# Sixteen offloaded quarter tiles spread over fourteen states, in place of four whole states, in a fused Mamba decoder kernel

## The chip, the cores and the metric

One core of one Trainium2 chip runs the whole program in a single launch. The metric is the device time of that launch in microseconds (us); the time before is the median of three runs. The engines are named as in the profile: PE is TensorE, PEld its weight loads, DVE VectorE, ACT ScalarE, POOL GpSimd and SP the queue that issues most DMAs.

## The reference, cut to what matters

A decoder layer over 4 sequences of 1024 tokens, width 512: a Mamba block with a gated MLP, a cross-attention, and a feed-forward layer with routed low-rank experts, each added to its input and layer-normalised. The change lies in the Mamba block's selective scan, which has 1024 channels and 16 states:

```python
dA = jnp.exp(jnp.einsum('bld,dn->bldn', dt, A))
dBu = jnp.einsum('bld,bln,bld->bldn', dt, Bm, u_act)
def step(h, inputs):
    dA_t, dBu_t = inputs
    h = dA_t * h + dBu_t
    return (h, h)
y = jnp.einsum('lbdn,bln->bld', hs, Cm) + u_act * Dp
```

The last line is the sum over the 16 states n of `hs * C`. Which engine adds which piece of that sum is all that the change touches. Everything is 32-bit.

## The kernel before, in words

**Blocks.** The 4096 tokens are cut into 8 chunks `c` of 512 tokens, and the 1024 channels into 2 halves of 4 blocks of 128. One chunk and one half make a group `g` of 16 states `n`; there are 16 groups, numbered 0 to 15. A group is even for the first half of its chunk and odd for the second half. So there are 256 state positions `k`, and each has four slots `q`. A slot is one call of `quarter(k, q, other)`. Every engine's instructions are chained in the order in which the program writes them (the wrapper `InOrder`, whose helper is line 289 of the profile). Only DMA issues on SP are placed by the tile scheduler.

**What a slot holds.** In slot (k, q) the program writes, in this order: four transposes on PE (`turn`, tile `ps_h`, 128 tokens of the four channel blocks of state k-1); some PE work of another stage (`other`); one scan on DVE (`scan`, 128x512, the q-th channel block of state k); one exponential on ACT (`exp`, tile `da`, for the scan two slots later; `da` has two buffers); `times_c` for the quarter tile t = q of state k-1, which multiplies the transposed tile by C and adds it to the accumulator `acc`; and in slots 0 and 1 a product on POOL (`times_b`, tile `hs`, 128x1024, half of the input of state k+1; `hs` has three buffers). From the second token chunk of a sequence on, ACT also adds the carried state to the first column of `hs`.

**Three ways of adding.** `times_c` takes one of these ways, by state:

- state 0: ACT writes `acc` (one instruction);
- state 15 (`JS`): ACT writes C times the tile into a buffer `hc`, and PE later sums `acc` and `hc` when it transposes back;
- states in `AS`: ACT writes `hc` (six buffers), and one slot later POOL adds `hc` to `acc`;
- all others: one DVE instruction, `acc = ps * c + acc`.

The POOL addition is put into phase 3 of the next slot, so it is queued after the product `times_b` that this slot holds. For t = 3 it lands between the two products of a position; for t = 0 behind the second; for t = 1 and 2 in slots that hold no product. As the sums of state n run one position late, a state n in `AS` frees DVE at position n+1: positions 5, 8, 11 and 14.

**The other stage.** In groups 0 and 1, `other` is the rest of the input projection. From group 2 on it is the MLP of the chunk before, metered at 1.9 units of PE work per slot; a unit is three matmuls (`ps_ab`, `ps_m`), one step of the output projection (`ps_o`) or four transposes (`ps_t`). The output projection of a chunk starts at a fixed slot, number 18 of an even group (position 4, slot 2), and takes 32 units. Behind it stands a chain over several engines: the sum of squares on ACT, a small reciprocal square root on POOL (`ss`, `rs_r`, `rs_w`, `nr`), a scaling on ACT (`hn`), transposes on PE (`ps_t`), and a split on ACT and DVE (`xn`). Each product pair of the MLP also gives DVE two instructions on `g`, ACT a tanh and a cast, and POOL a subtraction (`gs`).

**After the scan.** The last two chunks' MLP and the attention follow (from about 2577 us of the span). The change leaves their instructions as they are.

Of the kernel before, what the change touches and what calls it, by code (L numbers as in the profile page):

```python
# [126 lines left out]
LOADS = {(8, 0): [(0, 1), (0, 0)], (14, 1): [(1, 1)], (15, 0): [(1, 0)]}  # L127
FG = 4

AS = (4, 7, 10, 13)  # L130
JS = (15,)
H, DK, SK = 16, 32, 64
E, R = 8, 16
# [539 lines left out]
def scan_mlp(tc, cn, a, dr, before, bx, then):  # L673
# [8 lines left out]
    with ExitStack() as ctx, ExitStack() as sx:  # L682
# [12 lines left out]
        class Step:  # L695
# [79 lines left out]
            def times_c(self, t):  # L775

                c = cts[self.c][:, t, self.n : self.n + 1]
                ps = self.ps.rearrange("p i d -> p (i d)")
                if self.n == 0:
                    acc = accs[self.g, t] = ap.tile([P, GJ * P], F32, tag="acc", name="acc")  # L780
                    nc.scalar.activation(acc, ps, AF.Copy, scale=c)
                elif self.n in AS + JS:
                    acc = accs[self.g, t]
                    hc = yp.tile([P, GJ * P], F32, tag="hc", name="hc", bufs=6)
                    nc.scalar.activation(hc, ps, AF.Copy, scale=c)
                    if self.n in AS:
                        at(1, 3, nc.gpsimd.tensor_tensor, acc, acc, hc, ALU.add)
                    else:
                        hcs.setdefault((self.g, t), []).append(hc)
                else:  # L790
                    acc = accs[self.g, t]
                    nc.vector.scalar_tensor_tensor(acc, ps, c, acc, ALU.mult, ALU.add)
# [40 lines left out]
        def at(d, phase, f, *args):  # L833

            due.setdefault((now[0] + d, phase), []).append(lambda: f(*args))
# [218 lines left out]
        n = NC * 2 * NS  # L1054
# [961 lines left out]
```

## Time and profile before

| what | value |
|---|---|
| median of three runs | 3428.85 us (3427.82 to 3434.39) |
| profiled execution, its own time | 3433.46 us |
| its span | 3431.7 us |
| groups 0 and 1 (569.9 to 793.6 us) | 223.7 us |
| even groups 4 to 14, one each | 128.7 to 135.4 us |
| odd groups 3 to 15, one each | 121.0 to 124.7 us |

The profile is that of one execution. A group's bounds are the starts of its first scan and of the next group's first scan on DVE. An engine's busy time in a stretch is the union of its instructions; DVE instructions overlap a little at their ends, so the cost of one to the queue is the distance between starts. A wait is put down to what came last before the waiting instruction.

### The profile page before, as it was taken

To read this page: it belongs to the slowest core of one execution; us is meant where nothing else is said; L and a number is where in the kernel's file an instruction comes from. 1 tells how busy PE (TensorE), PEld (TensorE's weight loads), DVE (VectorE), ACT (ScalarE), POOL (GpSimd) and SP (SyncE) were. 2 spreads that over 40 slices of the span, in tenths; PEclk is the share of its full clock that TensorE was granted. 3 is DMA by queue.
4 is the path that set the end of the run, shared out by engine and by line. 5 is a ranking of instruction groups with operands and counts; after the bars stand their busy time and mean duration, and the time that the engine had idled before them with its cause. 6 is when DMAs were issued, how large, how long until landed. Compare 5 with 4: busy or idle time off the path is not lost. (4 is left out here: it accounts for less than half of the span.)

```text
span 3431.7 us, 46914 instructions
## 1 busy us (share of the span) xinstructions
PE 3015.1 (88%) x15504; PEld 2369.0 (69%) x15504; DVE 2962.6 (86%) x4169; ACT 1982.9 (58%) x3894; POOL 2487.0 (72%) x2177
## 2 busy tenths in 40 slices
PE   7888885567898899899899899899899997999986
PEld 5666663344775776776776776776776787998875
DVE  6989999999999998998998998998993446888887
ACT  4666666555665655665555665656662335666642
POOL 1455447898998998998998998998993115667642
PEclk9999996567998999999999999999999999999998
DMA  4666645333655765665755665765657642111110
GB/s 163 217 240 226 240 167 176 132 111 121 195 176 180 220 189 186 215 193 185 222 186 182 214 190 179 221 188 187 202 177 236 178 129 90 32 56 50 42 37 31
DMA packets 478473, 562.77 MB, mean 164 GB/s; under 512 B 46006, under 2 KB 309814, under 8 KB 477974
## 3 DMA queue, kind: packets, MB, share of 16 engines
q1 hardware_dynamic: 464406, 526.21, 48.0%
q10 hardware_dynamic: 13824, 33.56, 2.7%
q8 instruction: 123, 2.02, 0.2%
q14 instruction: 120, 0.98, 0.1%
HBM read 430.18 MB, written 129.50 MB: 163 GB/s over the span
## 5 line engine op out<-in xcount | busy, mean ns | idle before, releaser
L289 POOL TENSOR_TENSOR hs<-pk,b 128x1024 f32<-128x1024 f32 x512 | 1213.9, 2391 | 61.8 <-issue 26.3
L289 DVE TENSOR_TENSOR_SCAN hs<-da,hs 128x512 f32<-128x512 f32 x1024 | 1220.4, 1208 | 15.6 <-ACT da L289 14.5
L289 ACT ACTIVATE da<-pk,aneg 128x512 f32<-128x512 f32 x1024 | 706.9, 691 | 734.1 <-DVE hs L289 726.5
L289 PE MATMUL ps_h<-ident,hs 128*128 128x128 f32 x4096 | 716.5, 299 | 190.0 <-DVE hs L289 128.1
L289 PEld LDWEIGHTS ps_h<-ident,hs 128*128 128x128 f32 x4096 | 549.8, 153 | 432.6 <-DVE hs L289 158.1
L289 PE MATMUL ps_ab<-xn,w 128*128 128x512 f32 x3072 | 837.7, 408 | 4.0 <-DVE xs L289 3.4
L289 PEld LDWEIGHTS ps_ab<-xn,w 128*128 128x128 f32 x3072 | 546.8, 191 | 99.4 <-DVE xs L289 4.1
L289 DVE SCALAR_TENSOR_TENSOR acc<-ps_h,c,acc 128x512 f32<-128x512 f32 x640 | 465.3, 727 | 63.3 <-PE ps_h L289 49.7
L289 PE MATMUL ps_m<-w,gs 128*128 128x512 f32 x1536 | 424.0, 411 | 8.0 <-POOL gs L289 5.5
L289 POOL TENSOR_TENSOR acc<-acc,hc 128x512 f32<-128x512 f32 x256 | 325.6, 1286 | 39.2 <-ACT hc L289 39.1
L289 PEld LDWEIGHTS ps_m<-w,gs 128*128 128x128 f32 x1536 | 277.2, 193 | 59.8 <-POOL gs L289 8.9
L289 PE MATMUL ps_o<-wo,wy 128*128 128x512 f32 x512 | 242.4, 598 | 0.3 <-DMA wo<-in_w_out_dram 0.3
L289 POOL TENSOR_TENSOR gs<-g,gs 128x512 fp32r<-128x512 f32 x128 | 165.1, 1290 | 103.6 <-ACT gs L289 101.6
L289 ACT ACTIVATE hc<-ps_h,c 128x512 f32<-128x512 f32 x320 | 216.0, 675 | 17.5 <-PE ps_h L289 17.2
L289 PE MATMUL ps_in<-xn,wu 128*128 128x512 f32 x768 | 220.3, 436 | 0.7 <-ACT xn L450 0.4
L289 PE MATMUL ps_in<-xn,wz 128*128 128x512 f32 x768 | 192.2, 398 | 3.0 <-ACT wz L147 2.4
L289 PEld LDWEIGHTS ps_in<-xn,wu 128*128 128x128 f32 x768 | 148.8, 195 | 62.0 <-issue 25.5
L289 POOL TENSOR_TENSOR pt<-pw,pt 128x512 fp32r<-128x512 f32 x48 | 64.6, 1345 | 150.3 <-ACT pt L289 117.2
L289 PEld LDWEIGHTS ps_in<-xn,wz 128*128 128x128 f32 x768 | 142.6, 188 | 36.8 <-ACT wz L147 2.8
L289 DVE SCALAR_TENSOR_TENSOR g<-g,ps_ab 128x512 f32<-128x512 f32 x128 | 86.5, 676 | 85.4 <-ACT g L289 83.8
L289 DVE SCALAR_TENSOR_TENSOR cv<-ps_in,pvec,cv 128x509 f32<-128x509 f32 (+2 forms) x192 | 143.2, 746 | 4.8
L289 POOL TENSOR_TENSOR r<-r,e 128x512 f32<-128x512 f32 x64 | 92.1, 1444 | 68.8 <-DVE e L289 43.1
(247 smaller groups left out, 4891.5 us busy)
## 6 DMA issues: line engine op xcount, KB each, us to landing
w<-w SPq DMA_DIRECT2D x384, 512.0 KB, 5.3
b<-b SPq DMA_DIRECT2D x256, 256.0 KB, 4.0
pk<-pk SPq DMA_DIRECT2D x64, 512.0 KB, 7.4
w<-pt SPq DMA_DIRECT2D x48, 512.0 KB, 3.3
pk<-z SPq DMA_DIRECT2D x64, 256.0 KB, 2.2
pk<-u SPq DMA_DIRECT2D x32, 512.0 KB, 3.5
pk<-r SPq DMA_DIRECT2D x32, 512.0 KB, 3.9
pk<-q SPq DMA_DIRECT2D x32, 512.0 KB, 4.4
```

Of the source, the lines that this page charges most:

```text
L289: ins = f(*args, **kw)
```

## The change

`AS` becomes a set of pairs (state, quarter tile) in place of four states, and `times_c` looks up the pair:

```diff
-AS = (4, 7, 10, 13)
+
+AS = {(n, t) for n in range(1, 15) for t in range(4) if (4 * (n - 1) + t) * 16 % 56 < 16}
...
-                elif self.n in AS + JS:
+                elif (self.n, t) in AS or self.n in JS:
                     acc = accs[self.g, t]
                     hc = yp.tile([P, GJ * P], F32, tag="hc", name="hc", bufs=6)
                     nc.scalar.activation(hc, ps, AF.Copy, scale=c)
-                    if self.n in AS:
+                    if self.n not in JS:
                         at(1, 3, nc.gpsimd.tensor_tensor, acc, acc, hc, ALU.add)
```

The pairs are (1,0), (2,0), (2,3), (3,3), (4,2), (5,2), (6,1), (7,1), (8,0), (9,0), (9,3), (10,3), (11,2), (12,2), (13,1), (14,1): sixteen in each group, four for every t, as before. States 0 and 15 stay as they were. No instruction is added or removed on any engine; on DVE, ACT and POOL the ones of this sum change places, PE's order is the same, and on SP some loads swap with their neighbours.

## The prediction

> **What bounds the kernel now.** I read the engine shares first, then busy time by group, then by state position in an even and an odd group, then what DVE waits for, then single instructions on DVE and POOL. The page's line for DVE:
>
> ```profile
> DVE  6989999999999998998998998998993446888887
> ```
>
> Each digit is a fortieth of the span, in tenths. From slice 6 to slice 29, where the scan runs beside the other stages, DVE is at 8 or 9. The scan phase is therefore near DVE's limit, and what is left is in the eights. Busy time by group (columns: us, then PE, PEld, DVE, ACT, POOL busy with instruction counts, PE clock, DMA share, GB/s), for groups 8 to 11:
>
> ```profile
> 1548.50:1681.80 133.30, 118.93 (x585) 86.63 (x584) 120.78 (x143) 71.76 (x131) 116.74 (x83) 0.95 0.55 175
> 1681.80:1804.10 122.30, 117.19 (x650) 96.05 (x650) 119.00 (x139) 73.44 (x132) 115.10 (x75) 1.00 0.71 218
> 1804.10:1939.50 135.40, 120.81 (x586) 86.46 (x585) 121.24 (x144) 82.78 (x183) 117.33 (x85) 0.95 0.55 177
> 1939.50:2064.10 124.60, 117.36 (x650) 96.08 (x649) 119.03 (x139) 82.76 (x174) 114.70 (x72) 1.00 0.71 219
> ```
>
> DVE has the same work in both kinds. An odd group leaves it idle for 122.3 - 119.0 = 3.3 us: nothing but DVE bounds it. An even group leaves it idle for 133.3 - 120.8 = 12.5 us. That idle time is the stake. By state position, same columns, in group 8: positions 5 to 9, 11 and 12, and then position 5 of group 9:
>
> ```profile
> 1587.50:1592.60 5.10, 5.10 (x21) 2.75 (x20) 5.10 (x7) 4.14 (x9) 2.94 (x3) 1.00 0.82 237
> 1592.60:1603.00 10.40, 10.40 (x41) 5.56 (x40) 7.93 (x10) 4.30 (x9) 9.38 (x7) 1.00 0.12 36
> 1603.00:1610.70 7.70, 7.70 (x31) 4.21 (x30) 7.70 (x10) 3.35 (x8) 5.88 (x4) 1.00 0.11 36
> 1610.70:1616.80 6.10, 6.10 (x25) 3.32 (x24) 5.22 (x7) 4.44 (x10) 6.10 (x4) 1.00 0.08 29
> 1616.80:1627.90 11.10, 11.10 (x53) 7.49 (x52) 7.90 (x11) 4.91 (x10) 8.88 (x6) 1.00 1.08 317
> ...
> 1636.20:1642.20 6.00, 6.00 (x38) 5.06 (x36) 5.86 (x8) 5.09 (x11) 6.00 (x4) 1.00 0.54 164
> 1642.20:1655.50 13.30, 7.76 (x38) 6.03 (x35) 10.59 (x14) 7.12 (x13) 13.30 (x9) 0.74 0.20 60
> ```
> ```profile
> 1723.20:1728.80 5.60, 5.60 (x33) 4.62 (x32) 5.60 (x7) 4.03 (x8) 5.17 (x5) 1.00 0.30 102
> ```
>
> Positions 5, 8 and 11 are those where a whole state is off DVE. In the even group PE is busy for all of positions 5 to 9 (40.4 of 40.4 us): this is the output projection. There DVE runs through position 5 in 5.1 us and then waits at position 6; the same happens at 8 and 9. Two of the four offloaded states free DVE where PE is the bound. At positions 11 and 12 POOL is busy throughout (19.3 of 19.3 us). In the odd group DVE is busy for all of position 5, so an offload there is fully used. What DVE waited for in group 8 (waiting, what ended it, us, times, longest):
>
> ```profile
> DVE acc L289 <- PE ps_h L289: 7.2, 6, 2.9
> DVE acc L289 <- POOL acc L289: 2.3, 1, 2.3
> ```
>
> And the POOL one in order of time, first on DVE, then on POOL:
>
> ```profile
> 1633.14 0.72 DVE L289 SCALAR_TENSOR_TENSOR acc<-ps_h,c,acc 128x512 f32<-128x512 f32 x1
> 1633.78 1.21 DVE L289 TENSOR_TENSOR_SCAN hs<-da,hs 128x512 f32<-128x512 f32 x1
> ...
> 1642.18 1.22 DVE L289 TENSOR_TENSOR_SCAN hs<-da,hs 128x512 f32<-128x512 f32 x1
> 1645.72 0.75 DVE L289 SCALAR_TENSOR_TENSOR acc<-ps_h,c,acc 128x512 f32<-128x512 f32 x1 [2.31 <-POOL acc L289]
> ```
> ```profile
> 1639.76 4.71 POOL L289 TENSOR_TENSOR hs<-pk,b 128x1024 f32<-128x1024 f32 x2
> 1644.43 1.25 POOL L289 TENSOR_TENSOR acc<-acc,hc 128x512 f32<-128x512 f32 x1
> ```
>
> From these starts I take the cost of one sum to DVE's queue: 1633.78 - 1633.14 = 0.64 us (its record says 0.72, but its end overlaps the next start). The stall shows POOL, late, holding up the first sum of state 11.
>
> **The change, part by part.** Work is the same on every engine: 16 offloads a group, before and after. Only the places differ, so the sum goes by place.
>
> *Up to the output projection, even groups 2 to 14.* Before position 5, the old kernel had no offload. The new one has four: (1,0) runs at position 2, (2,0) and (2,3) at 3, (3,3) at 4. Positions 3 and 4 are DVE's (its busy time is all of 7.8 and 7.1 us in group 8), so three of these shorten them: 3 x 0.64 = 1.9 us. The one at position 2 I take as worth nothing: DVE waited there for PE anyway. The projection's start is fixed by slot, so it comes 1.9 us sooner. Inside, PE's pace holds: DVE needs about 7.1 + 0.7 - 0.6 = 7.2 us a position (four scan-and-sum pairs of 1.13 + 0.64, one MLP instruction, less one sum) against PE's four slots of 2.16 us between successive groups of `ps_h`, 8.6 us. Five offloads instead of eight lie there, and the three that leave cost nothing. 7 x 1.9 = 13.5 us gained. Bounds: 0, if the projection's start hangs on something else, to 7 x 2.6.
>
> *Behind the projection, even groups.* POOL's order up to the second product for position 12 was h, two products, `gs`, two products; it becomes h, two products, add, `gs`, product, add, product. Two adds of 1.25 us come ahead: the first product of position 12 ends at about 1643.4 instead of 1642.1, the second at 1647.0 instead of 1644.4. DVE loses three free sums at position 11 (one stays), so in group 8 it gets to position 12 at 1636.2 + 4 x 1.13 + 3 x 0.64 + 2 x 0.6 = 1643.9, just after the product. The sum that stalled is then ready, and the third scan of position 12 starts at about 1649.4; before, it started at 1650.15. That is 0.8 us gained in groups 4, 8 and 12. The same count in group 10, where DVE waited only 0.54 us for that add, gives 0.35 us lost in groups 6, 10 and 14. Together -1.3 us. One add fewer stands ahead of the `gs` that ended a wait of PE (1.36 us) at position 13, behind which DVE waited 0.67 to 0.78: I take 0.7 off in six groups, 4.2 us. Bounds a group: +1.8 (see the POOL rival) to -3.6 (all idle time of DVE from position 10 to 13 gone).
>
> *Odd groups.* DVE is busy nearly throughout, and 16 x 0.64 us are saved wherever they lie. PE must hold without DVE's fast positions: it needs 4 x 1.83 = 7.3 us a position (start to start of `ps_h` beside two MLP units), DVE 7.1 + 1.2 - 0.6 = 7.7 with two MLP instructions. POOL's products were ready 2.5 us or more ahead of their scans at positions 10 to 13, so one add more in between is covered. Value 0; bounds -1.5 (half of the idle 3.3) to +0.9 (three light positions at PE's pace).
>
> *Groups 0 and 1.* DVE is busy 218.3 of 223.7 us. Value 0, bounds -4 to +2.
>
> *ACT and SP.* ACT's sixteen `hc` (0.67 us) go from bursts of four to singles; ACT is busy below 70% in every group, and `da` has two slots of lead. If that cover failed, each would cost its 0.67 us on a scan. The swapped loads on SP are taken at nothing: no DMA heads a wait of DVE above 0.4 us in groups 8 and 9.
>
> [...] In the trace the adds took 1254/1289/1327 ns (least, median, most) and DVE's sums 720/723/753 between 1200 and 2400 us, so neither waits on the other. [...]
>
> *Sum.* -13.5 - 1.3 - 4.2 = -19 us. Against the profiled execution's own 3433.5 us (span 3431.7 and 1.8 around it) that is 3414.5. The median of the runs is 4.6 us lower, so I forecast 3428.85 - 19 = 3410 us, 0.55% less. Some 0.2%, 7 us, is what a measurement can tell from no change.
>
> **The rivals.** *Smoothing pays everywhere (0.12).* If no engine meets a burst any more, even groups lose 1.9 + 3.6 = 5.5 us and odd ones 1.5: 7 x 5.5 + 7 x 1.5 = 49, near 3380. For it: three engines each have 116 to 121 us of work in 133. Against: the projection stays PE's.
>
> *Nothing moves (0.15).* If POOL and PE, not DVE, set where the projection starts, the 13.5 us are not gained, and the rest is within 6 us. For it: POOL is busy for all of positions 1 and 2 of group 8. Against: positions 3 and 4 are all DVE.
>
> *POOL decides at positions 11 to 13 (0.22), slower.* The products have no lead there (first scan at 1636.22, product done just before). Two adds ahead and a third, (10,3), between the next two delay the chain by 3 x 1.25 = 3.75 us in each even group, against 1.9 gained: 7 x 1.85 = +13, 3442 us. It decides if POOL gets there more than 0.5 us later against DVE than I count.
>
> **How the numbers follow.** My forecast has 0.51. It spreads by 10 us, so 0.47 of it is a gain above 7 us and 0.04 none. With the first rival, faster is 0.59; with the second, the same is 0.19; the third makes slower 0.22. The range, 3384 to 3439, reaches from near the smoothing case to short of the POOL case; about 0.2 is left out.
>
> **What would show it.** Right: even groups shorter by about 2 to 3.5 us, odd ones within 1; positions 3 and 4 shorter by three sums; DVE's wait for POOL's `acc` gone; `ps_o` still without gaps. Wrong: waits of DVE or ACT for POOL's `hs` at positions 11 to 13, odd groups longer with DVE waiting for `ps_h`, or adds above 1.33 us.

## The result

The kernel after takes 3437.64 us (median of 20 runs, 3432.16 to 3440.41) against 3430.07 us for the kernel before on the same chip (20 runs): 1.0019 times the time before by the means, with an interval of 1.0012 to 1.0026. It is slower by some 6.5 us (7.6 us between the medians) where 19 us of gain were forecast.

The profiled execution of after took 3432.16 us, span 3430.4. It is the fastest of its runs. The scan phase (groups 0 to 15) grew from 2007.4 to 2012.7 us. What lies around it, the same instructions in both, took 1424.3 us in the one profile and 1417.7 in the other, and between 1417.7 and 1426.9 in all profiles of this study. So the profiles are used below for places, and the medians for what a kernel costs.

The page of after, DVE's row by fortieths of the span:

```profile
DVE  6989999998999998998999999999993446888887
```

The row is as full as before. Groups 8 to 11 by windows (us, then PE, PEld, DVE, ACT and POOL busy with instruction counts, PE clock, DMA share, GB/s):

```profile
1552.30:1686.00 133.70, 118.67 (x585) 86.94 (x584) 120.91 (x143) 72.08 (x131) 117.48 (x92) 0.96 0.56 178
1686.00:1809.60 123.60, 118.03 (x650) 96.00 (x649) 118.94 (x140) 72.83 (x132) 114.34 (x66) 1.00 0.69 215
1809.60:1943.90 134.30, 121.46 (x585) 89.08 (x584) 120.99 (x143) 82.95 (x183) 117.86 (x94) 0.92 0.57 178
1943.90:2067.60 123.70, 117.99 (x650) 96.02 (x649) 118.97 (x139) 81.96 (x174) 113.73 (x64) 1.00 0.70 218
```

The even groups still leave DVE idle for 12.8 and 13.3 us, the odd ones for 4.7: the idle time that was the stake is all there. The next windows are positions 4 to 9, 11, 12, 14 and 15 of group 8, then positions 3 and 5 of group 9:

```profile
1583.70:1590.10 6.40, 5.27 (x22) 4.26 (x23) 6.40 (x8) 3.36 (x6) 6.40 (x5) 0.73 0.77 261
1590.10:1597.90 7.80, 7.80 (x34) 4.55 (x33) 7.17 (x10) 5.29 (x10) 6.86 (x5) 1.00 0.66 199
1597.90:1606.40 8.50, 8.50 (x33) 4.46 (x32) 7.30 (x9) 3.81 (x8) 5.29 (x3) 1.00 0.12 39
1606.40:1614.20 7.80, 7.80 (x32) 4.28 (x31) 7.28 (x10) 3.70 (x8) 7.80 (x6) 1.00 0.04 15
1614.20:1622.80 8.60, 8.60 (x33) 4.59 (x32) 7.33 (x9) 4.15 (x9) 8.49 (x6) 1.00 0.24 55
1622.80:1631.30 8.50, 8.50 (x44) 6.11 (x43) 7.11 (x9) 3.60 (x8) 5.33 (x3) 1.00 1.09 325
...
1639.70:1649.80 10.10, 6.33 (x35) 4.51 (x34) 7.69 (x9) 4.80 (x10) 10.10 (x6) 1.00 0.64 181
1649.80:1659.90 10.10, 6.95 (x38) 5.88 (x37) 9.79 (x13) 7.35 (x14) 10.10 (x7) 0.83 0.18 50
...
1669.20:1677.60 8.40, 6.91 (x38) 5.34 (x37) 8.37 (x12) 3.50 (x6) 7.81 (x4) 1.00 0.85 291
1677.60:1686.00 8.40, 7.51 (x41) 6.06 (x40) 8.37 (x12) 3.90 (x7) 6.93 (x19) 1.00 0.92 308
...
1709.80:1719.30 9.50, 7.61 (x46) 6.17 (x44) 7.08 (x9) 3.59 (x7) 9.50 (x6) 1.00 1.10 326
...
1726.90:1734.60 7.70, 7.49 (x41) 6.02 (x41) 7.70 (x11) 4.54 (x8) 5.75 (x4) 1.00 0.37 124
```

Positions 5 to 9 are even now, and PE fills them (41.2 of 41.2 us; 40.4 before): the projection is still PE's. At position 11 DVE works for 7.69 of 10.10 us while POOL is full. At 14 and 15 DVE is full, as it was before, when the two took 15.6 us and not 16.8:

```profile
1666.30:1672.80 6.50, 6.01 (x35) 4.82 (x34) 6.47 (x10) 4.21 (x7) 4.36 (x4) 1.00 0.82 247
1672.80:1681.90 9.10, 8.21 (x45) 6.60 (x44) 9.06 (x14) 4.38 (x9) 8.45 (x11) 1.00 1.06 374
```

In group 9, position 5 is DVE's as before, but position 3 leaves it idle for 2.4 us. What DVE waited for in group 8:

```profile
DVE acc L290 <- PE ps_h L290: 5.3, 11, 1.4
DVE y L290 <- PE ps_y L290: 3.7, 3, 1.6
DVE acc L290 <- POOL acc L290: 2.4, 1, 2.4
DVE hs L290 <- POOL hs L290: 1.1, 1, 1.1
```

The wait for POOL's `acc`, 2.3 us before, is still there, with a wait for POOL's `hs` beside it. In order of time, DVE and then POOL:

```profile
1639.72 1.22 DVE L290 TENSOR_TENSOR_SCAN hs<-da,hs 128x512 f32<-128x512 f32 x1 [1.07 <-POOL hs L290]
1643.33 0.75 DVE L290 SCALAR_TENSOR_TENSOR acc<-ps_h,c,acc 128x512 f32<-128x512 f32 x1 [2.38 <-POOL acc L290]
```
```profile
1632.25 0.19 POOL L290 TENSOR_SCALAR ss<-ss 128x4 f32<-128x4 f32 x1 [4.12 <-ACT carry L290]
...
1636.04 1.29 POOL L290 TENSOR_TENSOR h<-h,hn 128x512 f32<-128x512 f32 x1
1637.29 4.76 POOL L290 TENSOR_TENSOR hs<-pk,b 128x1024 f32<-128x1024 f32 x2
1642.00 1.29 POOL L290 TENSOR_TENSOR acc<-acc,hc 128x512 f32<-128x512 f32 x1
```

The stall has moved one position ahead, from the first sum of state 11 to the first of state 10: it waits for the add of (9,0) into the same accumulator, which POOL reaches behind the norm's chain (`ss` to `nr`), `h` and two products.

Where the time went, by stretch of a group, as means of the seven profiled groups of a kind (starts of first scans, as in the views above):

| stretch | before | after | change | forecast |
|---|---|---|---|---|
| even, positions 0 and 1 | 12.88 | 13.47 | +0.59 | 0 |
| even, 2 to 4 | 25.23 | 23.34 | -1.89 | -1.9 |
| even, 5 to 9 (projection) | 40.60 | 41.09 | +0.49 | 0 |
| even, 10 to 13 | 37.96 | 37.71 | -0.25 | -0.8 |
| even, 14 and 15 | 15.37 | 16.62 | +1.25 | not counted |
| odd, 0 to 3 | 33.52 | 32.90 | -0.62 | 0 (whole group) |
| odd, 4 to 15 | 89.26 | 90.11 | +0.85 | |

The 0.59 us of positions 0 and 1 lie in groups 2 and 4 alone (2.2 and 2.0 us). Group 2 comes up again below; in group 4 DVE waits 1.7 us for ACT's `da`, which it did not before, and why stays open. The last group is counted up to the end of its last scan.

### The profile page after: what moved, and what is told of

Read it like the earlier page. It is cut to its first block, busy times and chain, and to the rows that moved or that the text cites. A ratio compares the mean times of both kernels' runs of the same rounds, so it can differ in the third digit from the quotient of the medians.

```text
span 3430.4 us, 46766 instructions
## 1 busy us (share of the span) xinstructions
PE 3012.5 (88%) x15504; PEld 2370.4 (69%) x15504; DVE 2961.4 (86%) x4169; ACT 1981.4 (58%) x3894; POOL 2486.5 (72%) x2177
## 4 chain that ended last, share of the span: by engine, by line
PE 39%; DVE 35%; issue 9%; DMA 7%; ACT 5%; POOL 4%; SPq 0%; ACTq 0%; DVEq 0%; POOLq 0%
DVE hs L290 12%; DVE acc L290 7%; PE ps_ab L290 7%; PE ps_o L290 7%; PE ps_m L290 5%; PE ps_in L290 4%; PE ps_h L290 4%; PE ps_s L290 3%; PE ps_b L290 2%; DVE g L290 2%; DVE cv L290 2%; POOL hs L290 2%; DMA uz<-pk 2%; DVE h L290 1%; PE ps_y L290 1%
```

## The experiments

Theory: the change is the sum of a gain ahead of the projection and of new waits behind single instructions in POOL's and SP's queues. Rivals, by run: the gain is not there; the loss is one and the same everywhere; POOL is simply full. A function `offload(g)` gives the set of pairs by group; WHOLE is the set of before and SPREAD that of after. All ratios are to the kernel before on the same chip; 0.001 is 3.4 us.

**Which groups lose.** Three runs with SPREAD in one kind of group only, WHOLE in the others.

```diff
-                elif (self.n, t) in AS or self.n in JS:
+                elif (self.n, t) in offload(self.g) or self.n in JS:
# x1_odd:   SPREAD if g > 2 and g % 2 else WHOLE
# x2_even:  SPREAD if g >= 2 and g % 2 == 0 else WHOLE
# x3_first: SPREAD if g < 2 else WHOLE
```

> The spread set in the odd groups from 3 on, whole states elsewhere. Theory A (odd groups are DVE's before and after, so it does not matter where the sixteen sums lie): within 3 us of the kernel before; the seven odd groups of the two profiles differ by +1.7 us together. Rival B (without whole states DVE loses its run ahead, and each position costs the greater of PE and DVE): 5 to 8 us slower, with waits of DVE for ps_h in the odd groups.

> The spread set in the even groups from 2 on, whole states elsewhere. Theory A (what positions 3 and 4 save is capped by PE, which runs there at a granted clock of about 0.75, and the stall on POOL's sum moves from position 12 to position 11): within 4 us of the kernel before. My forecast's reading was 19 us faster. Rival B (the whole loss of the changed kernel lies here): 5 to 8 us slower.

> The spread set in groups 0 and 1 alone, beside the input projection, whole states elsewhere. Theory A (POOL is late for its products in group 1 once single sums stand among them; the two profiles differ by +2.3 us there): 2 to 6 us slower, the greater part of what the changed kernel loses. Rival B (the loss lies in the even or odd groups): within 2 us of the kernel before.

Measured: x1 3439.46 us, 1.0027 (1.0016 to 1.0037); x2 3427.61, 0.9987 (0.9979 to 0.9996); x3 3436.70, 1.0019 (1.0009 to 1.0029). The even groups gain some 4 us (by the profiles nothing: +0.2 us a group in the table), far short of 19; the odd ones lose 9 and groups 0 and 1 lose 6, where the forecast had nothing. The three add up to 11 us against 6.5 for the whole change, within their intervals. Rival B of x1 has the sign and nearly the size, but not its cause: DVE's long wait in the odd groups of x1 is for a `uz` load (below), not for `ps_h`.

**The three early sums.** After, with (2,0), (2,3) and (3,3) left on DVE in even groups from 2 on.

```diff
+    return SPREAD - {(2, 0), (2, 3), (3, 3)} if g >= 2 and g % 2 == 0 else SPREAD
```

> The changed kernel, but in the even groups from 2 on the pairs (2,0), (2,3) and (3,3) stay on DVE. My forecast priced these three at 1.9 us a group: 13 us slower than the changed kernel. Theory A (PE, slow at positions 3 and 4, starts the projection only about half of that sooner): 3 to 7 us slower. Rival (the start hangs on PE alone): within 2 us.

Measured: 3445.56 us, 1.0046 (1.0033 to 1.0058), 0.0027 or 9.3 us more than after: 1.3 us a group. The gain ahead of the projection is real, at two thirds of its forecast size: more than the 3 to 7 us of theory A, less than the forecast's 13.

**Offloads inside the projection.** The kernel before, with states 4 and 7 wholly on DVE in even groups from 2 on: eight sums, 8 x 0.64 = 5.1 us more of DVE work a group.

```diff
+    return {(n, t) for n, t in WHOLE if n > 7} if g >= 2 and g % 2 == 0 else WHOLE
```

> The kernel before, but in the even groups from 2 on states 4 and 7 stay on DVE whole, so that only states 10 and 13 are offloaded there: DVE gets 8 x 0.64 = 5.1 us a group more. Theory A (their places, positions 5 and 8, lie in the stretch that the output projection paces on PE): within 4 us of the kernel before. Rival (every saved sum counts): 30 us slower or more.

Measured: 3428.61 us, 0.9991 (0.9982 to 1.0001). 36 us of DVE work more cost nothing: there PE sets the pace, and eight of the sixteen offloads of an even group were worth nothing in the kernel before.

**The add of (9,0).** After, with this one sum on DVE in even groups from 2 on.

```diff
+    return SPREAD - {(9, 0)} if g >= 2 and g % 2 == 0 else SPREAD
```

> The changed kernel, but in the even groups from 2 on the pair (9,0) stays on DVE, so that fifteen sums are offloaded there. Theory A (POOL reaches the add of (9,0) late, behind the square root and two products, and DVE's first sum of position 11 waits 2.4 us for it): that wait goes, DVE does 0.64 us more, 1 to 2 us a group less than the changed kernel, 7 to 14 us in all. Rival B (POOL's products set the pace there, whoever does the sum): within 3 us of the changed kernel, with DVE waiting for hs instead.

Measured: 3425.01 us, 0.9983 (0.9972 to 0.9994), 0.0036 or 12 us less than after. One offload fewer made the kernel faster. What DVE waited for in group 8 of x4 (the same view as for after):

```profile
DVE acc L296 <- PE ps_h L296: 5.4, 11, 1.4
DVE y L296 <- PE ps_y L296: 2.9, 2, 1.6
DVE hs L296 <- POOL hs L296: 0.7, 1, 0.7
```

No wait for POOL's `acc` is left. Positions 10 to 13 take 35.72 us in the mean, 2.0 less than after.

**The uz loads.** `y` of the group before is made at positions 1 to 4, and its four `uz` tiles have two buffers: loads 3 and 4 follow the first and second `y` product on POOL. In the kernel after, group 9, POOL's queue, then ACT's and DVE's:

```profile
1706.28 1.28 POOL L290 TENSOR_TENSOR acc<-acc,hc 128x512 f32<-128x512 f32 x1
1707.52 1.29 POOL L290 TENSOR_TENSOR y<-y,uz 128x512 f32<-128x512 f32 x1
```
```profile
1711.03 0.33 ACTq L290 DMA_DIRECT2D uz<-pk  x1
1717.52 0.75 DVE L290 SCALAR_TENSOR_TENSOR y<-uz,dhalf,ps_y 128x512 f32<-128x512 f32 x1 [2.42 <-PE ps_h L290]
```

The add of (1,0) now stands ahead of the second product; the load behind it leaves ACT's queue at 1711.03 and is needed at 1715. The view names PE for the wait; in x1, the same wait is put down to the load:

```profile
DVE y L296 <- DMA uz<-pk: 2.5, 1, 2.5
```

The add is only a part of this wait. The same load and the same `y` in the kernel before:

```profile
1705.20 0.37 ACTq L289 DMA_DIRECT2D uz<-pk  x1
1712.43 0.75 DVE L289 SCALAR_TENSOR_TENSOR y<-uz,dhalf,ps_y 128x512 f32<-128x512 f32 x1 [0.41 <-DMA uz<-pk]
```

DVE waited for this load already: 0.4 to 1.5 us in odd groups 5 to 15 of before, 1.5 to 2.4 us in after. Counted from the start of group 9, DVE now gets to this `y` after 29.1 us (30.2 before), so what it saved turns into waiting; and the load leaves after 25.0 us (23.4 before). The `y` product that releases the load ends after 22.8 us, no later than before (22.9; in x1 it is 24.1), because POOL enters these groups 0.7 to 1.4 us earlier in after. The rest of the delay in group 9 is ACT's queue, which held the load until an `h` load issued on SP had landed at 1710.94: in the trace ACT waits for semaphore 107, on which the landings of both loads count.

x8 is after with three loads at the group's start and only the fourth behind the first product; `hc` has five buffers in place of six. x13 is the same edit on the kernel before.

```diff
-hc = yp.tile([P, GJ * P], F32, tag="hc", name="hc", bufs=6)
+hc = yp.tile([P, GJ * P], F32, tag="hc", name="hc", bufs=5)
-uz = uzs[self.g, i] = yp.tile([P, 2, T], F32, tag="uz", name="uz")
+uz = uzs[self.g, i] = yp.tile([P, 2, T], F32, tag="uz", name="uz", bufs=3)
-                if i < 2:
-                    at(1, 3, self.load_uz, i + 2, nc.scalar)
+                if i < 1:
+                    at(1, 3, self.load_uz, i + 3, nc.scalar)
...
                 this.load_uz(1, nc.sync)
+                this.load_uz(2, nc.sync)
```

> The changed kernel with three buffers for uz instead of two: three of a group's four loads are issued early on SP, the fourth after the first gated product; hc has five buffers instead of six. Theory C (in the odd groups and in group 1 the sums saved at positions 2 and 3 are lost to the second pair of uz loads, which start only after POOL's y products, now queued behind an add): DVE's waits for uz at position 3, 1.5 to 2.4 us a group, go, and the kernel is 8 to 12 us faster than the changed one. Rival B (loss from PE's pace): within 3 us of the changed kernel.

> The kernel before, with the change of x8 alone: three uz buffers, three of the four uz loads of a group at its start, only the fourth behind the first y product; five hc buffers in place of six. In the kernel before, DVE's idle time at position 3 of odd groups is 0 to 0.5 us (1.4 in group 11). Theory (the loads are late because of the change: an add now stands ahead of the y product that releases them): little to gain here, 7 groups x 0 to 0.5 us, so -4 to +1 us against the kernel before. Rival (early loads are worth their 10 us in any kernel, and x8's gain says nothing of the change): -8 to -12 us.

Measured: x8 3426.68 us, 0.9988 (0.9979 to 0.9997), 0.0031 or 11 us less than after. x13 3425.30, 0.9990 (0.9981 to 0.9998), 3 us less than before, as the theory had it. So the early loads are worth 3 to 4 us in themselves, and 7 us of x8's gain are waiting that came with the change. Position 3 of group 9 in x8, the same window as above:

```profile
1709.80:1716.90 7.10, 7.10 (x44) 5.98 (x42) 7.10 (x10) 3.58 (x6) 7.10 (x5) 1.00 1.13 337
```

9.50 us have become 7.10, all DVE's.

**The pk load of groups 1 and 2.** POOL in the kernel after, at the end of group 1 (group 2 starts at 794.2 us), and what SP's DMA queue waited for from 782.2 to 801.8 us:

```profile
788.17 2.35 POOL L290 TENSOR_TENSOR hs<-pk,b 128x1024 f32<-128x1024 f32 x1
794.76 2.34 POOL L290 TENSOR_TENSOR hs<-pk,b 128x1024 f32<-128x1024 f32 x1 [4.24 <-DMA pk<-pk]
```
```profile
SPq L709 <- ACT carry L290: 7.2, 1, 7.2
```

At the end of groups 0 and 1 the scheduler now issues the second `pk0` load (for ACT's exponentials) ahead of the second `pk1` load (for POOL's products); before, it was the other way round. SP waits for ACT ahead of both, and they leave 6.2 and 5.7 us ahead of the next group's first scan; before, `pk1` left 10.2 us ahead, and POOL did not wait:

```profile
792.80 6.99 POOL L289 TENSOR_TENSOR hs<-pk,b 128x1024 f32<-128x1024 f32 x3
```

x14 moves only that `pk0` load to ACT's own queue, in these two groups.

```diff
-                nc.sync.dma_start(pk, dr["pk"][self.c][2 * self.half + jp][:, :, q])
+                eng = nc.scalar if self.g in (1, 2) and (jp, q) == (1, 0) else nc.sync
+                eng.dma_start(pk, dr["pk"][self.c][2 * self.half + jp][:, :, q])
```

> The kernel after, where one load changes its queue: for groups 1 and 2 the second pk0 load (input of ACT's exponentials) is issued by ACT instead of SP. In the kernel after, SP issues it ahead of the second pk1 load (input of POOL's products) at the end of groups 0 and 1, and waits there for ACT until 6.2 us before the next group's first scan; in the kernel before the pk1 load comes first, 10.2 us before. Theory (this swap on SP is the loss in groups 0 and 1: POOL waited 4.2 us for pk in the kernel after): the pk1 load leaves about 3 us earlier, POOL's wait for pk goes, group 1 takes 102 instead of 104.8 us and the first position of group 2 5.5 instead of 7.7 us: 4 to 6 us less than the kernel after. Rival (the loss is POOL's adds in the queue, the swap only follows from it): within 1.5 us of the kernel after.

Measured: 3433.42 us, 1.0009 (1.0001 to 1.0018), 0.0010 or 3.4 us less than after; the two intervals overlap, so the time alone leaves it open. The trace does not: POOL at the same place of x14, with group 2 starting at 794.0 us:

```profile
787.97 4.67 POOL L290 TENSOR_TENSOR hs<-pk,b 128x1024 f32<-128x1024 f32 x2
```

The two products follow each other without a wait. Group 1 takes 102.6 us (104.8 in after, 101.8 before) and the first position of group 2 4.8 us (7.7 and 5.5): 5.1 us in these two places.

**All three waits away.** After, with x4's, x8's and x14's edits together; every other sum stays where the change put it.

> The kernel after with three corrections at once: (9,0) left on DVE in even groups from 2 on (x4), three uz buffers with early loads (x8), and the pk0 load of groups 1 and 2 on ACT's queue (x14). The placing of all other sums is the change's. Theory (three separate waits, each behind one of POOL's or SP's queued instructions): they add up, 12 + 10 + 5 = 27 us less than the kernel after, near 3411 us. Rival (they share their cost: what one frees the next takes back): at most 15 us less, 3422 us or more.

Measured: 3403.03 us, 0.9924 (0.9911 to 0.9938), 0.0095 or 33 us less than after. The three alone gave 12 + 11 + 3 = 26 us: they do not share their cost. The 7 us above the sum lie within the intervals. Groups 8 to 11 of x15, the same windows as for after:

```profile
1536.90:1668.00 131.10, 117.79 (x585) 86.18 (x584) 121.40 (x145) 71.38 (x130) 116.19 (x91) 0.96 0.56 179
1668.00:1789.00 121.00, 117.53 (x650) 95.93 (x649) 118.78 (x139) 72.97 (x132) 114.17 (x66) 1.00 0.72 221
1789.00:1921.00 132.00, 118.25 (x586) 86.40 (x585) 121.48 (x145) 82.24 (x182) 116.76 (x94) 0.96 0.58 181
1921.00:2043.00 122.00, 117.62 (x650) 95.97 (x649) 118.81 (x139) 81.90 (x174) 113.66 (x64) 1.00 0.71 221
```

Every one is 1.7 to 2.6 us shorter than in after. Against x13 (before with the early loads) x15 is 22 us faster: the placing that the change makes, less (9,0), is worth about what the forecast said, once these waits are gone. That the two numbers agree is in part luck. By the profiles 16 of the 22 us lie in the even groups, where positions 10 to 13 are 2.4 us shorter (forecast 0.8) and 14 and 15 are 1.25 longer (not counted), and 6 us in the odd groups, where the forecast had none.

**Other places for the sums.** x9 keeps x4's even groups and, in groups 0, 1 and the odd ones, puts 16 sums into states 4 to 14 only, so that no add stands in POOL's queue while `y` is made.

```diff
+    if g >= 2 and g % 2 == 0:
+        return SPREAD - {(9, 0)}
+    return {(n, t) for n in range(4, 15) for t in range(4) if (4 * (n - 4) + t) * 16 % 44 < 16}
```

> Groups 0, 1 and the odd ones spread their sixteen sums over states 4 to 14, so that none is offloaded at positions 1 to 4; even groups from 2 on are as in x4_no90. Theory C: the odd groups and group 1 fall back to their length before or 0.5 us below, 8 to 10 us faster than x4_no90, about 15 us faster than the kernel before. Rival B (any spread costs the odd groups): within 3 us of x4_no90.

Measured: 3413.12 us, 0.9953 (0.9940 to 0.9965), 10 us less than x4, as theory C had it; the odd groups are 0.9 us shorter than in the kernel before. x10 takes x9's even groups, drops the five offloads of the projection and puts four at states 13 and 14, which run at positions 14 and 15; x11 is x10 with x8's loads; x12 is x10 with 18 offloads in odd groups.

```diff
-        return SPREAD - {(9, 0)}
+        return SPREAD - {(9, 0), (4, 2), (5, 2), (6, 1), (7, 1), (8, 0)} | {(13, 0), (13, 2), (14, 0), (14, 2)}
# x12, odd groups from 3 on:
+        return {(n, t) for n in range(4, 15) for t in range(4) if (4 * (n - 4) + t) * 18 % 44 < 18}
```

> x9 with other places in the even groups from 2 on: the five offloads that lie where PE paces the output projection, (4,2), (5,2), (6,1), (7,1), (8,0), go, and (13,0), (13,2), (14,0), (14,2) come, which run at positions 14 and 15, where DVE is the bound (busy 8.4 of 8.4 us, PE 6.9 and 7.5). 14 offloads a group in place of 15. Theory (an offload is worth 0.64 us where DVE is the bound and nothing in the projection's stretch): 7 groups x 4 x 0.64 = 18 us less at most; with PE next in line at 7.5 us after 0.9 us, 7 x 1.5 to 2.4 = 10 to 17 us less than x9, some 3398 to 3404 us. Rival (POOL is full at positions 14 and 15: four more adds of 1.29 us there hold up its products): within 3 us of x9 or slower.

> x10 with the three uz buffers of x8. Since no offload lies ahead of state 4 in odd groups, POOL's y products are as early as in the kernel before. Theory: the uz loads end no wait above 0.5 us there, so within 4 us of x10. Rival (early loads help in any kernel): -8 to -12 us against x10.

> x10 with 18 in place of 16 offloads in odd groups from 3 on, spread over states 4 to 14. Theory (DVE bounds every position from 4 on there): 7 x 2 x 0.64 = 9 us less than x10. Rival (POOL, busy 115 of 122 us and 2.5 us more with two adds, or PE at 7.3 us a position, takes over): within 3 us of x10 or slower.

Measured: x10 3427.96 us, 0.9998 (0.9989 to 1.0007), so 15 us slower than x9; x11 3412.33, 0.9950 (0.9937 to 0.9962); x12 3431.88, 1.0005 (0.9996 to 1.0014). The theory missed in all three. Dropping the five did nothing, as said (positions 5 to 9: 41.17 us, 41.30 in x9). The four late ones shortened the seven even groups by 17.5 us together, as said, and lengthened the seven odd ones by 31.1. POOL in x10 around the start of group 9 (1679.0 us), and DVE's wait there:

```profile
1677.58 1.28 POOL L298 TENSOR_TENSOR acc<-acc,hc 128x512 f32<-128x512 f32 x1
1678.94 0.23 POOL L298 TENSOR_SCALAR ln_v<-mv 128x4 f32<-128x4 f32 x1
...
1683.36 2.54 POOL L298 TENSOR_TENSOR acc<-acc,hc 128x512 f32<-128x512 f32 x2
1685.84 4.72 POOL L298 TENSOR_TENSOR hs<-pk,b 128x1024 f32<-128x1024 f32 x2
```
```profile
DVE y L298 <- issue: 3.7, 1, 3.7
DVE hs L298 <- POOL hs L298: 3.1, 1, 3.1
```

The layer norm's chain of sixteen small POOL instructions (4.4 us) starts behind the late adds, two more adds stand behind it, and the products of the new group come last. POOL then stays late up to the `y` products, and the `uz` loads with it. The one that `y` waits for here leaves 20.5 us after the group's start and lands after 29.2 (in group 9 of before it leaves after 16.3). This fits with the early loads being worth 16 us in x11 and 3 in x13. In x12 the even groups take 12.3 us more than in x10, and the odd ones only 3.4 less. DVE's waits there are for `y` again, in group 14 2.9 us for a `uz` load; that the two more adds are behind them is likely, but no run shows it.

**The best of these.** x9 with x8's loads, and WHOLE in groups 0 and 1.

```diff
 def offload(g):
+    if g < 2:
+        return WHOLE
```

> x9 with three uz buffers and, in groups 0 and 1, the four whole states of the kernel before. Theory: position 3 of odd groups loses its idle time (0.74 us in x13, 7 x 0.74 = 5 us) and groups 0 and 1 give back 0 to 4 us: 3404 to 3409 us. Rival (nothing adds to x9): within 3 us of x9's 3413.

Measured: 3403.88 us, 0.9926 (0.9913 to 0.9938), at the near end of what was expected, and level with x15. Both beat the kernel before by about 25 us and the kernel after by 32 to 33.

## Why the prediction was wrong

Much of what the text worked out from rows held in kind; what failed is each place where it took a cost at nothing or did not look.

*Up to the projection, -13.5: right, mis-sized.* Positions 2 to 4 are shorter by 1.89 us, as worked out. But the text took the projection's start to follow DVE one for one. In groups 6 to 14 it came 1.0 us sooner, and x5 gives 1.3 us a group: 9 us in all. What was late next was PE. In group 8 its first `ps_o` matmul now runs 1.2 us behind the start of position 5, before it was 0.4. The 0.49 us by which positions 5 to 9 grew are this remainder: in x5 they take 40.37 us again. PE at positions 4 and 5, where the two `ps_ab` lines are the same kind of three matmuls:

```profile
1586.01 1.52 PE L290 MATMUL ps_ab<-xn,w 128*128 128x512 f32 x3
...
1590.55 0.95 PE L290 MATMUL ps_ab<-xn,w 128*128 128x512 f32 x3
1591.34 1.02 PE L290 MATMUL ps_o<-wo,wy 128*128 128x512 f32 x2
```

Three matmuls take 1.52 us where the clock granted is 0.73 (the mean over position 4; 0.76 in the kernel before, so this is not new) and 0.95 us a little later, where it is 1.00. PE had waited 2.83 us for `acc` at position 3, its longest gap there, and worked 3.6 of the position's 7.3 us. Cut where the granted clock changes, these two stretches of the trace lead up to and hold the slow matmuls:

```profile
1582.71:1586.13 3.42, 1.45 (x11) 1.07 (x11) 3.42 (x4) 1.98 (x4) 3.42 (x3) 1.00 0.94 361
1586.13:1589.54 3.41, 3.41 (x13) 2.72 (x12) 3.41 (x5) 1.38 (x2) 3.41 (x3) 0.50 0.70 207
```

PE is busy for 1.45 us of the first, in which no gap reaches 1 us, and has half the clock (0.50) in all of the second. What lowered it there, no run shows.

*Inside the projection, 0: right* but for the late start above. x6, and the five that x10 dropped, show it from both sides.

*Behind the projection, -5.5: wrong sign.* Two things failed. First, the step followed POOL's order to position 12 and found the sum that had stalled ready. It did not ask which DVE sum comes next on the accumulator that a moved add writes: add (9,0) is followed by DVE's (10,0) on the same tile, at position 11, where POOL has no lead. That cost 2.4 us in group 8, and 12 us in all by x4. Without it positions 10 to 13 gain more than the text gave them: they are 2.2 us shorter than before in x4. The 0.7 us a group from one add fewer ahead of `gs` hardly show in after: DVE's waits for `ps_h` at positions 10 to 13 went from 0.8 to 0.3 us in group 8, stayed at 0.6 in group 12 and rose from 1.1 to 1.4 in group 10. Second, positions 14 and 15 were left out of the sum. There DVE is the bound (8.37 of 8.40 us), and the change takes four offloads away from position 14 and gives back one there and one at 15: 2 x 0.64 = 1.3 us a group, 1.25 measured, 8.8 in all. The text counted what leaves positions 5, 8 and 11, and not what leaves position 14.

*Odd groups, 0: wrong, +9 (x1).* By the profiles it is +7.4 in x1 and +1.6 in after, where POOL enters these groups earlier. "16 x 0.64 us are saved wherever they lie" failed at position 3: DVE is not the bound there, the `uz` load is, as it was by 0.4 to 1.5 us in the kernel before; the lines that the text read as "nothing but DVE bounds it" hide this wait in the 3.3 us of idle time. The three offloads that came to positions 2 and 3 should have saved 1.9 us and saved 0.6, and positions 4 to 15, which lost them, grew by 0.85. With the loads early (x15), position 3 takes 7.13 us in the mean instead of 8.80, and the odd groups are shorter than before by 1.4 each, near the bound of -1.5 that the text gave (0.6 of it comes with early loads alone, by x13). The claim that POOL's products have a lead that covers one more add held at positions 10 to 13; it does not hold for the `y` products in x1 (the second ends 24.1 us after the start of group 9, 22.9 before), which the step did not look at.

*Groups 0 and 1, 0: wrong, +6 (x3).* The bounds were -4 to +2. *ACT and SP at nothing: wrong on SP.* "No DMA heads a wait of DVE above 0.4 us" was read in groups 8 and 9 of before; the swap lies in groups 0 and 1, and its load heads a wait of POOL, not of DVE. The two failures are one: x14 takes back 3 to 5 us of these 6. What the rest is was not tried.

*Adds beside sums: right by the rows.* Between 1200 and 2400 us of after, POOL's adds take 1289 ns in the mean (152 of them) and DVE's sums 727 (377); before, it was 1287 and 728. Longer adds or sums have no part in this loss.

Of the rivals, "POOL decides at positions 11 to 13" came nearest in sign (3442 against 3437.64 us) and was right that POOL gets there too late. Its price was put on the products; most of it is on the add. It is a part of the story: the other waits lie in odd groups and at the start, where the text looked for none.

## What to carry to other kernels

When work is spread out, cost it in every queue where it lands: the next instruction behind each moved one, who waits for that one, and which load leaves only when it is done. Count the places that lose as carefully as those that gain, and read the order of DMA issues on every group that changes, not on two typical ones. A change that measures slightly slower may still hold its whole gain: here three small edits turned +6.5 us into -26, of which 3 would have come without the change.

## What was not expected

A `pk` load of 512 KB took 5.6 us from issue to landing (median of the four around the start of group 1) in the kernel before, and 7.5 us in x3, where the four leave nearer together. In after, the `pk1` load of group 2 left 5.7 us ahead of the group's first scan and took 6.2 us, so it was late by then.
